# Graph attention with one-hot counts: destination one-hots compared twelve chunks at a time, three source one-hots a block made by ScalarE

## The chip, the cores and the metric

The kernel runs on one core of a Trainium2 chip. A core has TensorE (PE, matrix products), VectorE (DVE), ScalarE (ACT, activations), GpSimd (POOL) and DMA queues that SyncE (SP) feeds. Each engine takes its own instructions in order; semaphores make one wait for another. The metric is the device time of one execution in microseconds, the median of three runs.

## The reference

The reference normalises 1250 rows of 768 values, sends them through two graph attention layers (eight heads of 128, then one head of 768), adds the result, and puts a feed-forward network with a routed part for six rows behind it. Cut to the attention layer that the change is about:

```python
h = (x @ W.T).reshape(n, heads, out_ch)
e = leaky_relu(a_src[src] + a_dst[dst], 0.2)          # one value per edge and head
m = segment_max(e, dst);  ex = exp(e - m[dst])
alpha = ex / (segment_sum(ex, dst)[dst] + 1e-16)
out = segment_sum(alpha[:, :, None] * h[src], dst)
```

There are 21250 edges, sorted by destination. The kernel doesn't work on edges: it counts, for each pair of destination and source, how many edges join them (a 1250 x 1250 matrix), and then computes attention densely with the counts as factors.

## The kernel before, in words

**Tiles.** Nodes are in 10 blocks of 125 (`NB`, `B`). Edges are in 170 chunks of 125 (`EC`), 17 to a block (`CPB`); edge j of a chunk sits on partition j. `src_f` and `dst_f` hold source and destination of each edge as columns, one per chunk.

**The count stage (0 to about 160 us).** `count_block(b)` accumulates in PSUM the count matrix of destination block b. For each chunk it needs two one-hot matrices, made by `hot_chunk`: `of`, 125 edges x 1250 sources, and `to`, 125 edges x up to 96 destinations. A matmul with `to` (32 columns of it, a quarter of the block) as weights and `of` as the moving matrix, in three column pieces of 512, 512 and 226, adds the chunk's edges to the quarter (L294). Since edges are sorted, each quarter only needs a window of chunks (`WINDOWS`, with a margin of two), and `steps_of` puts chunks of the four quarters side by side; from block 7 on there are twelve steps. A runtime check (`edges_outside`, `n_val`) guards the windows; its other branch, `count_all`, isn't run with these data.

`of` is a compare of the iota row `node` with a column of `src_f`, on VectorE (`one_hot`, L219), 170 of them. It is written to one of twelve slots of `ring`, or to a block of `absent` that isn't in use yet. `to` is a compare on GpSimd (63), on VectorE (10, in blocks 1 and 2), or on ScalarE in two instructions (97): Abs of node - dst (L273), then Relu of 1 - that (L276).

`use_count` evacuates a block: `full_w`, a copy of the counts to f16 on ScalarE (`act_copy`, L376); `absent`, a large value where there is no edge (ScalarE, L305); ten transposes on TensorE (L316) and two ScalarE copies to `ct`, the transposed counts. ScalarE does these in its own order with everything else it has.

**Beside the counts.** In block 0 the layer norm of x and the transposes to `xt` run. From block 3 on, each block issues one `h1_block` of head group 0 (six matmuls, L443, and a ScalarE copy), placed behind the newest count matmul with `issue_after`, and four maxima of `top_of_block` (eight in blocks 4 and 8 of the trace): VectorE subtracts `absent` from a row of source terms and takes the maximum (L557), which the softmax needs. After block 9 TensorE does the remaining h1 blocks, to about 200 us.

**Attention, from 200 us.** For each head and each of ten source blocks, `weights` makes a 125 x 1250 factor tile `pt` (three buffers): VectorE (L581), ScalarE's exp (L584), VectorE times the counts (L585). Ten matmuls (L749) use it. Between factors VectorE does the tops that are still open, of heads 5 to 7 for the most part (`top_steps`), and TensorE does h1 blocks of group 1 (in heads 0 to 3), `fold_att2` and `h2_part` matmuls (L726, from head 4 on). `finish_head` divides by the softmax sum and transposes (L661 to L675). Then come h2, the second layer (L905) and the feed-forward network.

**Order.** The program is written in the order above; a scheduler with priorities lays out each engine's list from it when the program is built, with tile buffers and `issue_after` as constraints. A changed tile or engine can therefore move other instructions of the same engine.

The lines that the change edits:

```python
to = ep.tile([B, 3 * QUART], BF16, tag="to", bufs=20, name=f"to{c}")
if c < 2 * CPB + MARGIN:
    eng = (nc.gpsimd, nc.scalar if c < CPB else nc.vector)[c % 2]
else:
    eng = (nc.gpsimd, nc.scalar, nc.scalar)[c % 3]
```

Of the kernel before, what the change touches and what calls it, by code (L numbers as in the profile page):

```python
# [25 lines left out]
F32 = mybir.dt.float32  # L26
BF16 = mybir.dt.bfloat16
F16 = mybir.dt.float16
I32 = mybir.dt.int32
U16 = mybir.dt.uint16  # L30
AF = mybir.ActivationFunctionType
OP = mybir.AluOpType
AX = mybir.AxisListType

N = 1250
# [7 lines left out]
B = 125  # L43
NB = N // B
EC = E // B
# [8 lines left out]
CPB = EC // NB  # L54
MARGIN = 2
QUART = 32
NQ = 4
# [10 lines left out]
def gnn_ffn(  # L68
# [25 lines left out]
    nc = tc.nc  # L94

    def pool(name, bufs=1, space=None, stack=ctx):
        if space is None:
            return stack.enter_context(tc.tile_pool(name=name, bufs=bufs, reuse_waits="tile"))
        return stack.enter_context(tc.tile_pool(name=name, bufs=bufs, space=space))
# [7 lines left out]
    def ps_mm(name):  # L107
        return mm_pool[0].tile([128, 512], F32, tag="mm", name=name)

    def ps_tr(name):  # L110
        return psum.tile([128, 512], F32, tag="tr", bufs=2, name=name)
# [16 lines left out]
    ep = pool("early", stack=early)  # L128
# [31 lines left out]
    for i in range(2):  # L160
# [3 lines left out]
    node = ep.tile([B, NW], F16, name="node")  # L164
    nc.gpsimd.iota(
        node, pattern=[[1, NW]], base=0, channel_multiplier=0, allow_small_or_imprecise_dtypes=True
    )
    src_f = ep.tile([B, EC], F32, name="src_f")
    nc.vector.tensor_copy(src_f, src_i)
    dst_f = ep.tile([B, EC], F32, name="dst_f")  # L170
    nc.vector.tensor_copy(dst_f, dst_i)
    minus_dst = ep.tile([B, EC], F32, name="minus_dst")
    nc.vector.tensor_scalar(minus_dst, dst_f, -1.0, None, op0=OP.mult)

    first_i = ep.tile([B, NB, CPB], I32, name="first_i")
    last_i = ep.tile([B, NB, CPB], I32, name="last_i")

    def quarters_of(r):

        return [  # L180
            NQ * o + j for o in (-1, 0, 1) for j in range(NQ)
            if WINDOWS[j][0] <= r - CPB * o < WINDOWS[j][1]
        ]

    def start_of(quarter):
        return quarter // NQ * B + quarter % NQ * QUART

    for t, bounds in (
        (first_i, [start_of(quarters_of(r)[0]) for r in range(CPB)]),
        (last_i, [start_of(quarters_of(r)[-1] + 1) for r in range(CPB)]),  # L190
    ):
        c0 = 0
        for c1 in range(1, CPB + 1):
            if c1 == CPB or bounds[c1] != bounds[c0]:
                nc.gpsimd.iota(
                    t[:, :, c0:c1], pattern=[[B, NB], [0, c1 - c0]], base=bounds[c0],
                    channel_multiplier=0,
                )
                c0 = c1

    absent = marks.tile([B, NB, N], BF16, tag="marks", name="absent")
    ct = gpool.tile([B, NB, N], U16, name="ct")
    ones = ep.tile([B, 1], F32, name="ones")
# [14 lines left out]
    def one_hot(t, col, nodes):  # L218
        return nc.vector.tensor_scalar(t, nodes, col, None, op0=OP.is_equal)  # L219
# [23 lines left out]
    ring = ep.tile([B, 12, N], BF16, name="ring")  # L243
# [7 lines left out]
    hot = {}  # L251
    newest = {}

    def hot_chunk(c):

        quarters = [q + c // CPB * NQ for q in quarters_of(c % CPB)]
        quarters = [q for q in quarters if 0 <= q < NQ * NB]
        of = place_of[c]
        newest["of"] = one_hot(of, src_f[:, c : c + 1], node[:, :N])
        n0 = start_of(quarters[0])  # L260
        w = start_of(quarters[-1]) + QUART - n0
        to = ep.tile([B, 3 * QUART], BF16, tag="to", bufs=20, name=f"to{c}")
        if c < 2 * CPB + MARGIN:
            eng = (nc.gpsimd, nc.scalar if c < CPB else nc.vector)[c % 2]
        else:
            eng = (nc.gpsimd, nc.scalar, nc.scalar)[c % 3]
        if eng is not nc.scalar:
            eng.tensor_scalar(  # L268
                to[:, :w], node[:, n0 : n0 + w], dst_f[:, c : c + 1], None, op0=OP.is_equal
            )  # L270
            return of, to, n0
        away = ep.tile([B, 3 * QUART], F16, tag="away", bufs=1, name=f"away{c}")
        nc.scalar.activation(  # L273
            away[:, :w], node[:, n0 : n0 + w], AF.Abs, bias=minus_dst[:, c : c + 1], scale=1.0
        )
        nc.scalar.activation(to[:, :w], away[:, :w], AF.Relu, bias=ones, scale=-1.0)  # L276
        return of, to, n0

    def count_block(b, between={}):


        p = ps_count(f"count{b}")
        for i, step in enumerate(steps_of(b)):
            for _, c, _, _ in step:
                if c not in hot:
                    hot[c] = hot_chunk(c)
            if i in between:
                between[i]()
            for c0 in range(0, N, 512):
                c1 = min(N, c0 + 512)  # L290
                for j, c, first, last in step:
                    of, to, n0 = hot[c]
                    o = start_of(NQ * b + j) - n0
                    newest["count"] = nc.tensor.matmul(  # L294
                        p[QUART * j : QUART * (j + 1), c0:c1], to[:, o : o + QUART], of[:, c0:c1],
                        start=first, stop=last,
                    )
        use_count(p[:B, :N], b, f"w{b}", F16)

    def use_count(c, b, name, kind=F32):  # L300


        full = ep.tile([B, N], kind, tag="full", bufs=1, name=f"full_{name}")
        act_copy(full, c)
        nc.scalar.activation(absent[:, b], full, AF.Relu, bias=big_pos, scale=-ABSENT)  # L305
        if kind == F32:
            transpose_blocks(
                lambda g, m: ct[:, g : g + m, b * B : (b + 1) * B],
                lambda i: full[:, i * B : (i + 1) * B],
                NB, B, B, 4, f"ctp_{name}", act_copy,  # L310
            )
            return
        for g in range(0, NB, NB // 2):
            p = psum.tile([128, 8, 128], F16, tag="tr", bufs=2, name=f"ctp_{name}_{g}")
            for i in range(NB // 2):
                nc.tensor.transpose(  # L316
                    p[:B, i, :B], full[:, (g + i) * B : (g + i + 1) * B], ident16[:B, :B]
                )
            act_copy(ct[:, g : g + NB // 2, b * B : (b + 1) * B], p[:B, : NB // 2, :B])
# [22 lines left out]

    def edges_outside():

        below = ep.tile([B, EC], F32, name="below")
        outside = ep.tile([B, EC], F32, name="outside")
        n_out = ep.tile([B, 1], F32, name="n_out")
        nc.vector.tensor_tensor(below, dst_f, first_i.rearrange("p b c -> p (b c)"), OP.is_lt)
        nc.vector.tensor_tensor(outside, dst_f, last_i.rearrange("p b c -> p (b c)"), OP.is_ge)
        nc.vector.scalar_tensor_tensor(  # L350
            outside, outside, 1.0, below, op0=OP.mult, op1=OP.add, accum_out=n_out
        )
        n_p = ps_tr("n_out_p")
        nc.tensor.matmul(n_p[:1, :1], n_out, ones, start=True, stop=True)
        n_i = ep.tile([1, 1], I32, name="n_i")
        nc.vector.tensor_copy(n_i, n_p[:1, :1])
        return nc.values_load(n_i[:1, :1], min_val=0, max_val=E)
# [7 lines left out]
    def transpose_blocks(dst_of, src_of, n, rows, cols, per, name, evac):  # L365

        for g in range(0, n, per):
            m = min(per, n - g)
            p = ps_tr(f"{name}_{g}")
            pv = p[:cols, : m * rows].rearrange("p (c j) -> p c j", c=m)  # L370
            for i in range(m):
                nc.tensor.transpose(pv[:, i, :], src_of(g + i), ident[:rows, :rows])  # L372
            evac(dst_of(g, m), pv)

    def act_copy(o, i):
        nc.scalar.activation(o, i, AF.Copy)  # L376
# [90 lines left out]
    p = ps_tr("vp")  # L467
# [19 lines left out]
    p = ps_mm("a1p")  # L487
# [117 lines left out]
    for b in range(1, NB):  # L605
        count_block(b)
        if b == 2:
            n_val = edges_outside()
        if b == 3:
            new_group()  # L610
        if b >= 3:
            with tc.issue_after(newest["count"].ins):
                h1_block(0, b - 3)
        first_tops(behind.get(b, ()), range(4))
        if b == 5:
            attention_columns()
            as1_lo, as1_hi = low_high(a1[:, 0], [B, H1, NB], "as1")
# [161 lines left out]
    p = ps_mm("a2p")  # L779
# [13 lines left out]
    p = ps_tr("a2tp")  # L793
# [101 lines left out]
    for q in range(NB // 2):  # L895
        pt = pt2[q]
        for i in range(2):
# [14 lines left out]
            for g in (1, 0):  # L912
                c = slice(g * 384, (g + 1) * 384)
# [4 lines left out]
        c = slice(2 * q, 2 * q + 2)  # L918
# [142 lines left out]
    for r1, r0 in ((0, 3), (1, 4), (2, None)):  # L1061
        pair = [(1, r1)] if r0 is None else [(1, r1), (0, r0)]
        for m in range(KH):
            for r, a in pair:
                for g in range(2):
                    q = 32 * (2 * (1 - r) + g)
# [6 lines left out]
    for r in range(2):  # L1073
        for g in range(2):
            q = 32 * (2 * (1 - r) + g)
            c = slice(g * 384, (g + 1) * 384)
# [67 lines left out]
```

## Time and profile before

| | us |
|---|---|
| median of three runs | 787.17 (786.72 to 787.53) |
| the profiled execution | 786.1 |
| its span, first to last instruction | 784.3 |
| TensorE busy | 745.2 |
| VectorE busy | 580.0 |
| ScalarE busy | 323.7 |
| GpSimd busy | 121.1 |
| block 8's and block 9's `full_w` start | 145.25, 157.40 |
| first attention matmul | 200.57 |

How to read it: "busy" sums the time in which an engine has an instruction running, so it says where the work is, not what waits for what. The chain that ended last follows the work back from the last instruction, at each step to what released it. A group's row gives line, engine and operation, output<-input with shape, how many, busy time and mean nanoseconds of one, then the idle time of the engine just before them and what ended it. A wait's row gives who waited for whom, the sum in us, how often, and the longest. Matmul rows count two records for each fp32 matmul.

### The profile page before, as it was taken

The page shows a single profiled execution, that of the slowest core. Times are in us where ns is not written, and L with a number is a line of the kernel's source. Part 1 is how long each engine was busy: PE and PEld are TensorE (multiplying, and loading weights), DVE is VectorE, ACT ScalarE, POOL GpSimd, SP SyncE. Part 2 cuts the span into 40 slices and gives each one's busy share as a digit, 9 for nine tenths or more (in the row PEclk, how much of TensorE's full clock was granted, in tenths as well). Part 3 has the DMA queues.
Part 4 walks back from the last instruction along what each step waited for, and adds up shares of the span by engine and source line. Part 5 has one row for each costly group of instructions (what it writes and reads, how often), then busy time and mean ns, then how long its engine had stood idle before and what let it go on. Part 6 is the DMA issues. An engine that isn't in the chain of part 4 may idle for free.

```text
span 784.3 us, 11527 instructions
## 1 busy us (share of the span) xinstructions
PE 745.2 (95%) x4612; PEld 493.4 (63%) x4612; DVE 580.0 (74%) x974; ACT 323.7 (41%) x589; POOL 121.1 (15%) x104
## 2 busy tenths in 40 slices
PE   4988998999989999899999999999999999999997
PEld 1553443544777777788888888455555555576755
DVE  7859999999999999999878785297856622251412
ACT  4989987522355546453635462202331300011000
POOL 5236677200000000000000000100010101023010
PEclk9999999899999999999999999999999999999999
DMA  9651000017002020422220100402211001094811
GB/s 238 217 207 41 3 1 1 2 67 242 37 2 67 1 67 1 147 81 67 81 67 1 67 1 2 152 0 69 64 36 31 29 20 40 0 316 111 329 40 40
DMA packets 21553, 58.49 MB, mean 75 GB/s; under 512 B 2385, under 2 KB 7627, under 8 KB 20344
## 3 DMA queue, kind: packets, MB, share of 16 engines
q1 hardware_dynamic: 21496, 57.72, 22.3%
q8 instruction: 37, 0.61, 0.3%
q14 instruction: 20, 0.16, 0.1%
HBM read 53.74 MB, written 3.98 MB: 74 GB/s over the span
## 4 chain that ended last, share of the span: by engine, by line
PE 60%; DVE 13%; issue 3%; ACT 2%; ACTq 0%; DVEq 0%
PE acc L905 15%; PE h2p L726 13%; PE acc L749 12%; DVE pt L581 6%; PE f L970 5%; PE f L954 5%; DVE pt L585 5%; PE h1p L443 4%; DVE unused L557 2%; PE h1tp L674 1%; ACT on L671 1%; PE a2p L782 1%; PE xt2p L372 1%; PE candp L1067 1%; PE v2p L696 1%
## 5 line engine op out<-in xcount | busy, mean ns | idle before, releaser
L584 ACT ACTIVATE pt<-pt,as_lo 125x1250 f32<-125x1250 f32 (+1 forms) x130 | 128.0, 1012 | 202.7 <-DVE pt L581 188.1
L749 PEld LDWEIGHTS acc<-g,pt 125*125 125x125 f32 x1600 | 185.0, 188 | 25.3 <-DVE pt L585 17.5
L749 PE MATMUL acc<-g,pt 125*125 125x129 f32 x1600 | 191.8, 275 | 7.1 <-DVE pt L585 7.1
L585 DVE SCALAR_TENSOR_TENSOR pt<-pt,ct 125x1250 f32<-125x1250 f32 (+1 forms) x130 | 133.2, 1053 | 11.9 <-ACT pt L584 11.5
L905 PE MATMUL acc<-h,pt 125*125 125x385 f32 (+1 forms) x400 | 129.7, 486 | 0.0
L581 DVE SCALAR_TENSOR_TENSOR pt<-rows_h,as_hi 125x1250 f32<-125x1250 f32 x80 | 119.8, 1514 | 11.0 <-PE acc L749 10.8
L443 PE MATMUL h1p<-w1s,xt 128*125 128x512 f32 x240 | 109.2, 597 | 0.6 <-ACT g L376 0.5
L905 PEld LDWEIGHTS acc<-h,pt 125*125 125x125 f32 x400 | 74.6, 187 | 53.9
L726 PE MATMUL h2p<-w2s,g 128*125 128x384 f32 x320 | 107.4, 487 | 0.0
L268 POOL TENSOR_SCALAR to<-node,dst_f 125x64 bf16<-125x64 f16 (+4 forms) x63 | 80.1, 1471 | 50.7 <-PE count L294 48.7
L726 PEld LDWEIGHTS h2p<-w2s,g 128*125 128x125 f32 x320 | 58.1, 187 | 37.7 <-issue 0.9
L294 PE MATMUL count<-ring,to 125*32 125x512 bf16 (+1 forms) x729 | 69.6, 362 | 6.4 <-DVE ring L219 5.3
L443 PEld LDWEIGHTS h1p<-w1s,xt 128*125 128x125 f32 x240 | 42.7, 188 | 47.4 <-issue 45.6
L294 PEld LDWEIGHTS <-to 125*32 125x32 bf16 x1068 | 37.7, 99 | 53.6 <-issue 23.8
L901 POOL TENSOR_TENSOR xb<-xb,b2r 125x768 f32<-125x768 f32 x10 | 18.5, 1850 | 326.0 <-DVE a_row L787 180.4
L219 DVE TENSOR_SCALAR ring<-node,src_f 125x1250 bf16<-125x1250 f16 x116 | 59.7, 545 | 7.0 <-PE count L294 4.5
L294 PE MATMUL count<-absent,to 125*32 125x512 bf16 (+1 forms) x339 | 52.4, 361 | 8.8 <-POOL to L268 6.6
L557 DVE CUSTOM_DVE_ANT_0 unused<-rows,absent 125x1250 bf16<-125x1250 f32 x40 | 58.0, 1449 | 0.4 <-DVEq L622 0.3
L557 DVE CUSTOM_DVE_ANT_0 unused<-srow_h,absent 125x1250 bf16<-125x1250 f32 x40 | 58.1, 1452 | 0.2
L974 DVE TENSOR_TENSOR o<-f,o 125x384 f32<-125x384 f32 x20 | 11.1, 557 | 52.5 <-PE f L970 27.4
L970 PE MATMUL f<-wf,gt 128*125 128x384 f32 x120 | 39.5, 486 | 0.0
L276 ACT ACTIVATE to<-away,ones 125x64 bf16<-125x64 f16 (+4 forms) x97 | 33.9, 349 | 13.3 <-PE count L294 9.4
(176 smaller groups left out, 619.5 us busy)
## 6 DMA issues: line engine op xcount, KB each, us to landing
rows_h<-r_h_d SPq DMA_DIRECT2D x8, 1250.0 KB
w_more<-in_atom_in_t SPq DMA_DIRECT2D x3, 1152.0 KB
w_more<-in_atom_out_t SPq DMA_DIRECT2D x3, 1152.0 KB
x<-in_x SPq DMA_DIRECT2D x10, 336.0 KB
xb<-in_x SPq DMA_DIRECT2D x10, 336.0 KB
srow_h<-as_d SPq DMA_DIRECT2D x5, 625.0 KB
w1n<-in_w SPq DMA_DIRECT2D x2, 1536.0 KB
w1s<-in_w1t SPq DMA_DIRECT2D x2, 1536.0 KB
```

Of the source, the lines that this page charges most:

```text
L219: return nc.vector.tensor_scalar(t, nodes, col, None, op0=OP.is_equal)
L268: eng.tensor_scalar(to[:, :w], node[:, n0 : n0 + w], dst_f[:, c : c + 1], None, op0=OP.is_equal)
L294: newest["count"] = nc.tensor.matmul(p[QUART * j : QUART * (j + 1), c0:c1], to[:, o : o + QUART], of[:, c0:c1], start=first, stop=last,)
L443: nc.tensor.matmul(p[:B], xt[:, k, b * B : (b + 1) * B], w1s[g][:, k], start=(k == 0), stop=(k == KD - 1),)
L557: nc.vector.tensor_tensor_reduce(out=unused, in0=hd.src_row, in1=absent[:, b], scale=1.0, scalar=-ABSENT, op0=OP.subtract, op1=OP.max, acc ...
L581: nc.vector.scalar_tensor_tensor(o, hd.rows[:, 0, c0:c1], hi, hd.rows[:, 1, c0:c1], op0=OP.add, op1=OP.max)
L584: nc.scalar.activation(o, o, AF.Exp, bias=lo, scale=1.0)
L585: nc.vector.scalar_tensor_tensor(o, o, 1.0, ct[:, s, c0:c1], op0=OP.min, op1=OP.mult)
L726: nc.tensor.matmul(p[:B, :384], groups[i][:, h, b * B : (b + 1) * B], w2h[i][:, h, g * 384 : (g + 1) * 384], start=(h == 0), stop=(h == 3),)
L749: nc.tensor.matmul(acc[g][:B, j * (C1 + 1) : (j + 1) * (C1 + 1)], pt[:, d * B : (d + 1) * B], h1v[h // 4][:, h % 4, s, :], start=(s == 0 a ...
L905: nc.tensor.matmul(acc[g][:B, : c1 - c0], pt[:, s, i * B : (i + 1) * B], h2[:, s, c0:c1], start=(s == 0), stop=(s == NB - 1),)
L970: nc.tensor.matmul(p[:B, :384], gt[:, m, i, :], wf2[:, m, c], start=(m == 0), stop=(m == KH - 1),)
```

## The change

A block's chunks are numbered r = 0 to 16. For the twelve chunks of `AT_ONCE`, whose destinations all fall in a window of 64, VectorE makes the destination one-hots in one compare per block, 125 x 768 elements: the row `near` (0 to 63) repeated, against twelve columns of `dst_near` (destination minus the start of the window), each repeated 64 times. The other five chunks' `to` are all on GpSimd. In blocks 3 to 9, chunks 4, 9 and 13 have their source one-hot made by ScalarE, Abs and then Relu over 1250 columns, instead of by VectorE. `minus_dst` goes, two tiles of `edges_outside` become bf16, and the unused branch of `use_count` takes its buffer from `ring`.

```diff
-    minus_dst = ep.tile([B, EC], F32, name="minus_dst")
-    nc.vector.tensor_scalar(minus_dst, dst_f, -1.0, None, op0=OP.mult)
...
+    AT_ONCE = (2, 3, 4, 5, 7, 8, 9, 10, 11, 12, 13, 14)
+    near = ep.tile([B, 2 * QUART], F16, name="near")
+    nc.gpsimd.iota(
+        near, pattern=[[1, 2 * QUART]], base=0, channel_multiplier=0,
+        allow_small_or_imprecise_dtypes=True,
+    )
+    dst_near = ep.tile([B, NB, len(AT_ONCE)], F16, name="dst_near")
+    for r0, r1, i in ((2, 6, 0), (7, 15, 4)):
+        nc.vector.tensor_sub(
+            dst_near[:, :, i : i + r1 - r0],
+            dst_f.rearrange("p (b c) -> p b c", c=CPB)[:, :, r0:r1], first_i[:, :, r0:r1],
+        )
...
+    def destinations_at_once(b):
+        t = ep.tile([B, len(AT_ONCE), 2 * QUART], BF16, tag="to_near", bufs=2, name=f"near{b}")
+        near_of[b] = t
+        shape = [B, len(AT_ONCE), 2 * QUART]
+        nc.vector.tensor_tensor(
+            t, near.unsqueeze(1).to_broadcast(shape),
+            dst_near[:, b].unsqueeze(2).to_broadcast(shape), OP.is_equal,
+        )
...
+        if r in AT_ONCE and b not in near_of:
+            destinations_at_once(b)
         of = place_of[c]
-        newest["of"] = one_hot(of, src_f[:, c : c + 1], node[:, :N])
+        if b >= 3 and r in (4, 9, 13):
+            away = ep.tile([B, N], F16, tag="away", bufs=1, name=f"away{c}")
+            nc.scalar.activation(
+                away, node[:, :N], AF.Abs, bias=src_f[:, c : c + 1], scale=-1.0
+            )
+            nc.scalar.activation(of, away, AF.Relu, bias=ones, scale=-1.0)
+        else:
+            newest["of"] = one_hot(of, src_f[:, c : c + 1], node[:, :N])
+        if r in AT_ONCE:
+            return of, near_of[b][:, AT_ONCE.index(r)], b * B + start_of(quarters_of(r)[0])
         n0 = start_of(quarters[0])
         w = start_of(quarters[-1]) + QUART - n0
-        to = ep.tile([B, 3 * QUART], BF16, tag="to", bufs=20, name=f"to{c}")
-        if c < 2 * CPB + MARGIN:
-            eng = (nc.gpsimd, nc.scalar if c < CPB else nc.vector)[c % 2]
-        else:
-            eng = (nc.gpsimd, nc.scalar, nc.scalar)[c % 3]
-        if eng is not nc.scalar:
-            eng.tensor_scalar(
-                to[:, :w], node[:, n0 : n0 + w], dst_f[:, c : c + 1], None, op0=OP.is_equal
-            )
-            return of, to, n0
-        away = ep.tile([B, 3 * QUART], F16, tag="away", bufs=1, name=f"away{c}")
-        nc.scalar.activation(
-            away[:, :w], node[:, n0 : n0 + w], AF.Abs, bias=minus_dst[:, c : c + 1], scale=1.0
-        )
-        nc.scalar.activation(to[:, :w], away[:, :w], AF.Relu, bias=ones, scale=-1.0)
+        to = ep.tile([B, 3 * QUART], BF16, tag="to", bufs=10, name=f"to{c}")
+        nc.gpsimd.tensor_scalar(
+            to[:, :w], node[:, n0 : n0 + w], dst_f[:, c : c + 1], None, op0=OP.is_equal
+        )
         return of, to, n0
...
-        full = ep.tile([B, N], kind, tag="full", bufs=1, name=f"full_{name}")
+        if kind == F32:
+            full = ring[:, 2:4].rearrange("p i n -> p (i n)").bitcast(F32)
+        else:
+            full = ep.tile([B, N], kind, tag="full", bufs=1, name=f"full_{name}")
...
-        below = ep.tile([B, EC], F32, name="below")
-        outside = ep.tile([B, EC], F32, name="outside")
+        below = ep.tile([B, EC], BF16, name="below")
+        outside = ep.tile([B, EC], BF16, name="outside")
```

## The prediction

> **What bounds the kernel now.** I read the page's busy shares first, then the chain that ended last, then a table by stage, then the waits and groups of the stage that the change edits. Share and chain:
>
> ```profile
> PE 745.2 (95%) x4612; PEld 493.4 (63%) x4612; DVE 580.0 (74%) x974; ACT 323.7 (41%) x589; POOL 121.1 (15%) x104
> PE 60%; DVE 13%; issue 3%; ACT 2%; ACTq 0%; DVEq 0%
> ```
>
> TensorE is busy 95% of the span, so there is little to win unless its idle time or the order of its work changes. The table by stage shows where that idle time is:
>
> ```profile
> core 0: us, PE busy (x) PEld busy (x) DVE busy (x) ACT busy (x) POOL busy (x), PEclk, DMA share, GB/s
> 0.00:56.00 56.00, 41.52 (x438) 21.23 (x442) 40.88 (x117) 41.09 (x87) 19.46 (x44) 0.94 0.68 213
> 56.00:160.00 104.00, 94.59 (x972) 47.53 (x961) 103.44 (x194) 82.57 (x193) 64.83 (x39) 0.97 0.05 19
> 160.00:200.00 40.00, 39.37 (x93) 16.92 (x92) 39.50 (x69) 10.41 (x13) 0.17 (x1) 1.00 0.45 153
> 200.00:330.00 130.00, 122.85 (x864) 100.61 (x863) 129.28 (x136) 64.38 (x85) 0.12 (x1) 1.00 0.14 48
> 330.00:560.00 230.00, 228.55 (x1370) 169.12 (x1369) 179.52 (x241) 95.45 (x158) 3.61 (x2) 1.00 0.17 55
> ```
>
> The change edits the count stage, which ends with the tenth block's count at 157.4 us. From 56 us on VectorE has no gap there (103.44 of 104), and it stays full to 330. TensorE is full from 160 to 200 (h1 blocks), waits for VectorE's attention factors from 200 to 330, and has no gap from 328 on. So VectorE microseconds saved before 160 come out at the end only through TensorE's start into attention, or through factors that arrive earlier between 200 and 330. The waits of 56 to 160, and the chain where VectorE hands over to TensorE:
>
> ```profile
> POOL to L268 <- PE count L294: 31.8, 10, 6.6
> ACT to L276 <- PE count L294: 9.4, 4, 6.7
> ACT full_w L376 <- PE count L294: 6.6, 3, 5.6
> PEld L294 <- ACT to L276: 3.9, 8, 0.7
> PE count L294 <- DVE ring L219: 3.0, 3, 1.5
> ```
>
> ```profile
> 323.58 2.95 DVE pt L581 x2
> 328.03 4.67 PE acc L749 x40
> ```
>
> GpSimd waits 31.8 us for TensorE: not a bound. ScalarE waits 16 us for TensorE, so it has room on average, not necessarily at each place. The durations that I use, by groups kept apart by shape:
>
> ```profile
> L219 DVE TENSOR_SCALAR ring<-node,src_f 125x1250 bf16<-125x1250 f16 x116 | 59.7, 545 | 7.0 <-PE count L294 4.5 <-PE vt L455 2.5
> L557 DVE CUSTOM_DVE_ANT_0 unused<-rows,absent 125x1250 bf16<-125x1250 f32 x40 | 58.0, 1449 | 0.4 <-DVEq L622 0.3
> L273 ACT ACTIVATE away<-node,minus_dst 125x64 f16<-125x64 f16 x70 | 24.3, 347 | 5.1 <-DVE minus_dst L173 3.1
> L305 ACT ACTIVATE absent<-full_w,big_pos 125x1250 bf16<-125x1250 f16 x10 | 13.3, 1329 | 0.0
> L376 ACT ACTIVATE full_w<-count 125x1250 f16<-125x1250 f32 x10 | 12.0, 1203 | 6.6 <-PE count L294 6.6
> ```
>
> Back to back, starts are nearer than durations: 0.457 us for a one-hot, 1.38 for a top, 0.38 for a ScalarE instruction of 64 columns, 1.1 for full_w.
>
> [...] a GpSimd one-hot takes 0.72 us beside an idle VectorE and 2.16 (median) from 56 to 160. [...]
>
> **The change part by part.** (1) VectorE, before 56 us. minus_dst (-0.17) goes; two small subtractions (+0.27) and block 0's compare come. A compare has 768 columns: from the trace's two-source 125x170 instruction, 0.24 from start to start[...]. Sum +0.96, ahead of the layer-norm scale that ScalarE waits for, but ScalarE no longer makes 0.38 us instructions in pairs there (minus_dst alone cost it 3.1 of waiting): nil or better. Blocks 1 and 2: two compares (1.73) for ten VectorE destination one-hots (1.7): nil. full_w of blocks 1 and 2 no longer queues behind ScalarE pairs (TensorE waited 2.58 and 1.85 there): the saturated phase starts about 0.4 earlier.
> (2) VectorE, blocks 3 to 9: ScalarE takes 21 source one-hots; 20 fall into the gap-free phase: -20 x 0.457 = -9.1. Compares: +6 x 0.865 = +5.2. Net -3.9. [...]
> (3) ScalarE per block: before, about 11.3 pairs x 0.76 = 8.6, plus full_w, absent, two ct copies and the h1 copy, 4.0: 12.6. After, 3 x (1.33 + 1.36) = 8.1 plus 4.0: 12.1. Blocks last 12.2 to 20.3 us, so it fits in total. But the pieces are long, and the instruction order of the changed kernel, fixed when the program is built, puts the ninth and thirteenth chunk's pair behind the previous block's full_w, absent, ct and h1 copy. With T the start of full_w, the third one-hot ends at about T + 8.3 (blocks 5, 7) and T + 9.4 (6, 8); TensorE needs it at T + 8.7 to T + 10. In block 9 the list is full_w 1.1, Abs 1.36, absent 1.33, ct 1.26, h1 copy (not before TensorE's h1 block at T + 6.0) 0.6, Relu, Abs, Relu 4.1: T + 10.7. TensorE wants it in the sixth of twelve steps, T + 8.7, so some 2 us are lost; the remaining steps take 3.6: the count ends at T + 14.3 where before it was 12.15.
> (4) Sum of the stage. Block 8's count: 145.25 - 0.4 - 18 x 0.457 + 6 x 0.865 = 141.8, with 0.4 lost to slots 142.2; block 9's: 142.2 + 14.3 = 156.5 against 157.40. TensorE then does the same 40 us of h1 blocks; its first attention matmul moves from 200.57 to 199.6: -0.97. VectorE's own gain is not lost at once (it has done more tops by then), but its fourth factor needs a buffer that TensorE's first attention group frees (it waited 0.19 for that at 202.97), so both start 0.97 early.
> (5) What moves later. The last 24 tops still have to be done between the factors (22 in the changed kernel, two more before the first). In the instruction order, tops done ahead of a factor, counted on from the kernel before's first factor (before / after): factor 30 15/15, factor 32 15/17, 40 18/21, 44 19/23, 50 24/24. Up to four tops (4 x 1.38 = 5.5 us) move from head 4, where VectorE has slack (1.7 to 3.8 us), into heads 2 and 3 and the start of 4, where TensorE waits for it; in TensorE's order three h2 matmuls and the att2 fold move ahead a little as filler. I wrote both orders forward with the trace's steps (factor parts 1.43 and 1.39, exp 1.1, top 1.38, an attention matmul 0.22, h2 0.645, h1 0.867), three factor buffers and six PSUM buffers. For before this puts head 7's first transposition at 493.6; the trace has 492.4. TensorE's idle in each stretch, before to after: 230 to 265 1.7 to 1.35, 265 to 350 8.3 to 11.5, 350 to 500 4.9 to 4.3. Net +2.2; with durations varied by a few hundredths, +1.9 to +2.6. After head 4 the two orders are the same work, TensorE gap-free.
> (6) bf16 for the two outside-edge tiles, the iota on GpSimd, fewer buffers: no wait in the trace stands on them, nil; with GpSimd late at the start, +0.3 at most.
> Sum: -0.97 + 2.2 = +1.2. On the profiled 786.1 (span 784.3 and 1.8 around it) 787.3; the median of the runs is 1.07 higher, so 787.17 + 1.2 = 788.4.
>
> **The rivals.** A, likeliest: as above, 788.4, own range 786.5 to 790; for it speaks the gap-free TensorE from 328, against it that a wait of 2 us in block 9 is read off a list. B, the saving survives: no ScalarE wait in block 9, its count ends at 153.5 (-3.9), and the compare costs less or the tops move harmlessly (+0.5 to +1.5): -2.4 to -4, about 784. It needs the count's end before 153.6; for it, the 103.44 of 104, against it the order in (5). B', block 9 without a wait but (5) as reckoned: -1.5, 785.7. C, slower: ScalarE sets the pace. Blocks 5, 6, 7 and 9, four tops each, took 51.6 together. If the third one-hot lands at T + 10.4 instead of T + 8.3 to 9.4 (a longer wait for the single away buffer, or a later h1 copy), each takes 14.0, 56.0 together: +4.4, less 1.9 saved elsewhere (0.4 at the start, and nine one-hots against three compares in blocks 3, 4 and 8): the count ends 2.4 later, with (5) +4.6, 791.8. It decides from 13.4 a block, where the count's end no longer comes earlier. A fourth, nothing reaches the end: VectorE idles the gain away in front of 200.57 and (5) costs half: 788.
>
> **How the numbers follow.** A 0.45, B 0.15, B' 0.10, C 0.25, nothing 0.05. About 0.2% (1.57 us) is what a measurement can tell from no change, 785.6 to 788.7. A lies 0.25 within and 0.20 above; B faster; B' 0.05 and 0.05; C slower; the last within. Faster 0.20, same 0.35, slower 0.45. The likeliest is 788.4; 8 in 10 reaches from B's upper part, 784.3, to C, 791.8.
>
> **What would show it.** The compare's row at about 0.87 from start to start, six of them in the saturated phase; 1250-wide Abs and Relu at 1.33; full_w of block 8 near 142 and of block 9 near 156.5 with a wait of TensorE for ScalarE's one-hot in block 9; first attention matmul near 199.6; TensorE's waits for factors between 265 and 350 up by about 3. It is wrong if block 9's count ends before 154 (then B or B'), if blocks 5 to 8 show TensorE waiting for ScalarE each time (C), or if waits from 265 to 350 are no longer than now.

## The result, and the profile after

The changed kernel takes 789.14 us (median of 17 executions, 787.51 to 791.79) against 787.53 for the kernel before in the same comparison (786.05 to 788.86): a ratio of 1.0023, with a 95% interval of 1.0013 to 1.0033. It is slower by about 1.8 us. 788.4 was predicted. The profiled execution took 787.51, the shortest of the 17; its span of 785.7 is 1.4 above the one before, and the readings below account for that 1.4, not for the 1.8 of all executions.

Shares and chain of the changed kernel (in its listing every line number after the count stage is 26 higher: L775 is L749, L583 is L557, L607 and L611 are L581 and L585):

```profile
PE 743.4 (95%) x4612; PEld 497.0 (63%) x4612; DVE 578.3 (74%) x954; ACT 312.3 (40%) x437; POOL 103.4 (13%) x92
...
PE 62%; DVE 11%; issue 3%; ACT 2%; ACTq 0%; DVEq 0%
```

VectorE lost only 1.7 us of busy time in all. The table by stage, columns as before the change:

```profile
0.00:56.00 56.00, 43.22 (x490) 21.76 (x490) 44.66 (x117) 31.53 (x51) 22.57 (x43) 0.97 0.67 208
56.00:160.00 104.00, 92.93 (x919) 49.98 (x919) 101.20 (x180) 82.38 (x78) 44.14 (x28) 0.93 0.06 22
160.00:200.00 40.00, 39.38 (x106) 17.94 (x105) 39.45 (x68) 9.75 (x12) 0.17 (x1) 1.00 0.45 153
200.00:330.00 130.00, 120.21 (x844) 99.85 (x844) 128.57 (x137) 63.77 (x84) 0.12 (x1) 0.99 0.14 48
```

Two things stand out. VectorE has done 44.66 us of work by 56 us, 3.8 more than before: it got going earlier. And between 200 and 330 TensorE is busy 2.6 us less than before while VectorE is as full as it was: TensorE waits more for it there.

The milestones say where the time went. Block 8's full_w starts at 140.37 (before 145.25), block 9's at 154.89 (157.40), the first attention matmul at 198.05 (200.57). So 2.5 us are saved where attention begins. A factor is one `pt` tile; they are numbered 0 to 79 over the eight heads, and a time given for one is the start of its first attention matmul. The lead holds to factor 16 (251.50 against 254.01) and is lost between factors 18 and 44: factor 24 is 2.06 ahead, but with three h1 matmuls still to do that the kernel before has behind it there; at factor 28, with those done, the lead is 0.07; factor 36 is 1.59 late, factor 44 1.46 late (355.99 against 354.53), and that stays to the end of the heads (492.23 against 490.81). After 200 us 3.9 us are lost. TensorE's waits for factors between 200 and 350 us (sum, how often, longest), in the kernel before and in the changed one:

```profile
PE acc L749 <- DVE pt L585: 7.1, 9, 1.5
```

```profile
PE acc L775 <- DVE pt L611: 9.7, 7, 3.0
```

The new operations cost what was reckoned. By groups kept apart by shape:

```profile
L271 DVE TENSOR_TENSOR near<-near,dst_near 125x768 bf16<-125x768 f16 x10 | 9.5, 953 | 0.0
...
L286 ACT ACTIVATE away<-node,src_f 125x1250 f16<-125x1250 f16 x21 | 28.0, 1335 | 1.9 <-POOL near L201 1.6
```

The compare has 0.87 from its start to the next instruction's (64.77 to 65.64), and the ScalarE instructions 1.34.

### The profile page after: what moved, and what is told of

It reads as the page before. It is cut to its first block, busy times and chain, and to the rows that moved or that the text cites. A ratio compares the mean times of both kernels' runs of the same rounds, so it can differ in the third digit from the quotient of the medians.

```text
span 785.7 us, 11306 instructions
## 1 busy us (share of the span) xinstructions
PE 743.4 (95%) x4612; PEld 497.0 (63%) x4612; DVE 578.3 (74%) x954; ACT 312.3 (40%) x437; POOL 103.4 (13%) x92
## 4 chain that ended last, share of the span: by engine, by line
PE 62%; DVE 11%; issue 3%; ACT 2%; ACTq 0%; DVEq 0%
PE acc L931 15%; PE acc L775 14%; PE h2p L752 13%; PE f L996 5%; PE f L980 5%; PE h1p L469 5%; DVE pt L607 5%; DVE pt L611 4%; DVE unused L583 2%; PE h1tp L700 1%; PE a2p L808 1%; ACT on L697 1%; PE xt2p L398 1%; PE v2p L722 1%; PE candp L1093 1%
## 5 line engine op out<-in xcount | busy, mean ns | idle before, releaser
L775 PEld LDWEIGHTS acc<-g,pt 125*125 125x125 f32 x1600 | 186.4, 189 | 26.9 <-DVE pt L611 16.8
L775 PE MATMUL acc<-g,pt 125*125 125x129 f32 x1600 | 192.4, 276 | 9.8 <-DVE pt L611 9.7
L611 DVE SCALAR_TENSOR_TENSOR pt<-pt,ct 125x1250 f32<-125x1250 f32 (+1 forms) x130 | 133.5, 1054 | 13.3 <-ACT pt L610 12.8
L607 DVE SCALAR_TENSOR_TENSOR pt<-rows_h,as_hi 125x1250 f32<-125x1250 f32 x80 | 120.3, 1514 | 13.2 <-PE acc L775 13.1
L297 POOL TENSOR_SCALAR to<-node,dst_f 125x61 bf16<-125x61 f16 (+4 forms) x50 | 62.9, 1361 | 57.6 <-PE count L317 52.4
L317 PE MATMUL count<-ring,near 125*32 125x512 bf16 (+1 forms) x474 | 55.4, 373 | 4.7 <-DVE ring L230 2.2
L583 DVE CUSTOM_DVE_ANT_0 unused<-rows,absent 125x1250 bf16<-125x1250 f32 x40 | 58.1, 1452 | 0.4 <-DVEq L648 0.3
L583 DVE CUSTOM_DVE_ANT_0 unused<-srow_h,absent 125x1250 bf16<-125x1250 f32 x40 | 58.1, 1454 | 0.2
L317 PE MATMUL count<-ring,to 125*32 125x512 bf16 (+1 forms) x255 | 52.2, 362 | 2.9 <-DVE ring L230 2.9
L317 PEld LDWEIGHTS <-near 125*32 125x32 bf16 x720 | 32.8, 103 | 34.0 <-issue 19.9
L230 DVE TENSOR_SCALAR ring<-node,src_f 125x1250 bf16<-125x1250 f16 x99 | 50.3, 543 | 4.3 <-PE count L317 4.3
L317 PE MATMUL count<-absent,near 125*32 125x512 bf16 (+1 forms) x246 | 42.2, 384 | 10.1 <-DVE near L271 7.1
L317 PEld LDWEIGHTS <-to 125*32 125x32 bf16 x348 | 28.5, 101 | 18.1 <-issue 9.1
```

The source lines that it names most:

```text
L297: nc.gpsimd.tensor_scalar(to[:, :w], node[:, n0 : n0 + w], dst_f[:, c : c + 1], None, op0=OP.is_equal)
L317: newest["count"] = nc.tensor.matmul(p[QUART * j : QUART * (j + 1), c0:c1], to[:, o : o + QUART], of[:, c0:c1], start=first, stop=last,)
L583: nc.vector.tensor_tensor_reduce(out=unused, in0=hd.src_row, in1=absent[:, b], scale=1.0, scalar=-ABSENT, op0=OP.subtract, op1=OP.max, acc ...
L607: nc.vector.scalar_tensor_tensor(o, hd.rows[:, 0, c0:c1], hi, hd.rows[:, 1, c0:c1], op0=OP.add, op1=OP.max)
L611: nc.vector.scalar_tensor_tensor(o, o, 1.0, ct[:, s, c0:c1], op0=OP.min, op1=OP.mult)
L775: nc.tensor.matmul(acc[g][:B, j * (C1 + 1) : (j + 1) * (C1 + 1)], pt[:, d * B : (d + 1) * B], h1v[h // 4][:, h % 4, s, :], start=(s == 0 a ...
```

## The experiments

In each comparison below the kernel before was run again beside the variant. Its medians were 786.52 in the comparison of the first four, 787.62 in that of the next four and 787.17 in the last, so ratios are the safer figure. Halved stretches are those in which the trace shows half the granted TensorE clock.

**1. The changed kernel with the tops where the kernel before has them.** The count stage is the changed one. Each top from the seventh of heads 5 to 7 on is tied behind one factor part:

```diff
             if s in top_steps.get(h, ()):
-                tops.pop(0)()
+                n = 3 * NB - len(tops)
+                if n in BEHIND:
+                    k, part = BEHIND[n]
+                    with tc.issue_after(factor[k][part].ins):
+                        tops.pop(0)()
+                else:
+                    tops.pop(0)()
```

> The changed kernel, with the tops of the attention stage held behind the same factor parts as in the kernel before, so that VectorE's list from the first factor on is that of before; the count stage is the changed one. Theory (order): the count stage's gain of 2.5 us reaches the first attention matmul, and the loss of 3.9 us after it comes from the tops' new places; then the first attention matmul stays near 198.0, every factor stays about 2.5 ahead of before, and the time is 2.5 below before, some 785.0, about 4 below the changed kernel. Rival (the clock, or where tiles lie): the loss of 3.9 stays with the old order, and the time is that of the changed kernel, 789.

Measured: 783.04, ratio 0.9956 (0.9942 to 0.9969). The first attention matmul is at 197.53, and the lead over the kernel before is 3.0 at every factor from 0 to 70, without a step. TensorE's waits for factors between 200 and 350 are as before:

```profile
PE acc L813 <- DVE pt L611: 7.1, 9, 1.5
```

So the loss after 200 us goes with the order of the tops, and the count stage's gain is real. From the first attention matmul on TensorE's list is that of the kernel before again too, instruction by instruction; in the changed kernel some h1 and h2 matmuls and a few attention matmuls stand elsewhere. The run puts both lists back at once and doesn't separate them.

**2. The kernel before with the tops as early as the changed kernel has them.**

> The kernel before with nothing of the change, but with the tops of the attention stage issued as early as the changed kernel has them (eight ahead of the first factor, the others behind and ahead of the same factor parts; some factor parts swap places with it, so the list is near to the changed kernel's but not the same). Theory (order): the count stage is as before, the first attention matmul stays at 200.6, and the time rises by 2 to 5 us (written forward as in the prediction this list costs 3.9): 790 to 792. Rival: the order of the tops costs nothing, 787.5.

Measured: 796.19, ratio 1.0121 (1.0105 to 1.0136), 9.7 above. The direction is the theory's, the size is twice what was expected. Of the 10.9 us by which its last attention matmul is late, 1.3 are there at the first one, 6.5 are more waiting of TensorE (13.6 against 7.1), and two halved stretches of 3.4 us, at 275.0 and 350.0, may make up most of the rest. This list was not the changed kernel's own (factor parts trade places in it, and head 7's source row is loaded earlier), so the run shows that a list of this kind is dear, not what this change's order costs.

**3. Tops in the old order, and block 9's third one-hot on VectorE.**

```diff
-        if b >= 3 and r in (4, 9, 13):
+        if b >= 3 and r in ((4, 9, 13) if b < 9 else (4, 9)):
```

> As the run with the tops held in the old order, and in block 9 the one-hot of chunk 13 is VectorE's again (ScalarE keeps chunks 4 and 9). Theory: TensorE's wait of 1.9 us for ScalarE's third one-hot in block 9 goes, VectorE pays 0.46 for it, the tenth count ends about 1.5 earlier (153.4), and so does the run: 783.5. Rival: the wait passes to the next late thing in that block (a VectorE one-hot, or the second of ScalarE): no difference from that run, 785.0.

Measured: 781.15, ratio 0.9941 (0.9928 to 0.9955). ScalarE's timeline of the changed kernel, block 9 (start, duration, instruction, and in brackets the idle time before it and what ended it), and the one TensorE row that waits in it:

```profile
140.37 1.21 ACT L402 ACTIVATE full_w<-count 125x1250 f16<-125x1250 f32 x1
141.47 1.33 ACT L286 ACTIVATE away<-node,src_f 125x1250 f16<-125x1250 f16 x1
142.70 1.32 ACT L331 ACTIVATE absent<-full_w,big_pos 125x1250 bf16<-125x1250 f16 x1
143.93 1.26 ACT L402 ACTIVATE ct<-ctp_w 125x625 uint16<-125x625 f16 x2
146.34 0.60 ACT L402 ACTIVATE g<-h1p 125x512 f32<-125x512 f32 x1 [1.15 <-PE h1p L469]
147.03 1.34 ACT L289 ACTIVATE ring<-away,ones 125x1250 bf16<-125x1250 f16 x1
148.40 1.34 ACT L286 ACTIVATE away<-node,src_f 125x1250 f16<-125x1250 f16 x1
149.77 1.34 ACT L289 ACTIVATE ring<-away,ones 125x1250 bf16<-125x1250 f16 x1
154.89 1.21 ACT L402 ACTIVATE full_w<-count 125x1250 f16<-125x1250 f32 x1 [3.78 <-PE count L317]
```

```profile
151.16 0.39 PE L317 MATMUL count<-ring,near 125*32 125x512 bf16 x2 [1.88 <-ACT ring L289]
```

The order is the predicted one: the third one-hot ends 10.7 after block 8's full_w, TensorE waits 1.88 for it, and block 9 takes 14.52. In the run without that third one-hot:

```profile
139.20 1.21 ACT L402 ACTIVATE full_w<-count 125x1250 f16<-125x1250 f32 x1
...
145.86 1.34 ACT L289 ACTIVATE ring<-away,ones 125x1250 bf16<-125x1250 f16 x1
...
151.52 1.21 ACT L402 ACTIVATE full_w<-count 125x1250 f16<-125x1250 f32 x1 [4.32 <-PE count L317]
```

Block 9 takes 12.32 here, 2.2 less, and nothing else took the wait's place. The median fell by 1.9 against the first run; the intervals of the two ratios overlap, so the size rests on the two profiles.

**4. Tops in the old order, all source one-hots on VectorE.** The condition on ScalarE's one-hots is never met (`b >= NB`).

> As the run with the tops held in the old order, but all source one-hots are VectorE's again: the compare of twelve chunks alone. Theory (VectorE's sum sets the count stage): 20 one-hots of 0.457 come back (9.1) and ScalarE's waits in block 9 go; against before VectorE has 5.2 more, less 0.4 to 1 at the start: the tenth count ends 4 later than before, near 161.5, and the time is 791.5. Rival (TensorE or ScalarE set the stage, the compare is hidden): within 1.5 of before.

Measured: 789.04, ratio 1.0037 (1.0024 to 1.0049), first attention matmul 202.89, 2.3 later than before. The theory's sign holds, its 4 was too much. Blocks 1 and 2 end at 48.50 and 56.39, 1.7 and 3.2 earlier than before, where 0.4 to 1 had been allowed. What TensorE waited for between 29 and 57 us, before and here:

```profile
PE ctp_w L316 <- ACT full_w L376: 2.6, 1, 2.6
PE xtp L372 <- ACT xt L376: 0.7, 1, 0.7
```

```profile
PE ctp_w L342 <- ACT full_w L402: 1.4, 1, 1.4
```

The new way of making destination one-hots is thus worth 3 us at block 2 by itself. That ScalarE's part in it counts most is read from these waits and not shown alone: the same edit takes ten destination one-hots off VectorE in blocks 1 and 2, and the kernel before has a halved stretch in block 2 (51.0 to 54.4) that this run doesn't have.

**5. Only the last six tops held.** The changed kernel, with `BEHIND` of the first run cut to tops 24 to 29.

> The changed kernel, its count stage untouched; of the tops of the attention stage only the last six are held behind the factor parts where the kernel before has them (factors 43 to 49), the others stay where the changed kernel puts them. Theory (the tops moved out of head 4 carry the loss): the time falls to that of the run with all tops in the old order, 783, or a little lower; written forward this list is 2.0 better than the old one: 781. Rival (the earlier tops, of heads 0 to 2, carry it): 787 to 789.

Measured: 784.6, ratio 0.9964 (0.9950 to 0.9977). From factor 28 to 44 this run gains 2.0 on the kernel before, where the changed kernel loses 1.5: that is the part that the tops moved out of head 4 carry. From factor 18 to 28 it still loses, as the changed kernel does. So the loss has two places, and neither the theory nor the rival had it whole. The second is at factor 20, where the new list puts the first part of factor 22 ahead of the second part of factor 21, and TensorE has no h1 matmul to do meanwhile. TensorE's timeline there, the changed kernel first, then the kernel before:

```profile
267.92 0.79 PE L775 MATMUL acc<-g,pt 125*125 125x129 f32 x2 [2.98 <-DVE pt L611]
```

```profile
267.12 2.49 PE L749 MATMUL acc<-g,pt 125*125 125x129 f32 x18 [1.00 <-DVE pt L585]
```

And around it the granted clock (the third column from the end) of the changed kernel:

```profile
262.00:267.00 5.00, 2.63 (x22) 2.24 (x20) 5.00 (x9) 1.82 (x2) 0.00 (x0) 1.00 0.00 0
267.00:271.00 4.00, 3.08 (x14) 3.08 (x15) 3.70 (x4) 3.17 (x10) 0.00 (x0) 0.57 0.00 0
271.00:276.00 5.00, 5.00 (x47) 4.93 (x46) 4.77 (x5) 3.75 (x7) 0.00 (x0) 1.00 0.01 3
```

In the four microseconds after the wait TensorE had 0.57 of its clock; one attention matmul (two records) takes 0.79 there. In this fifth run the halved stretch at the same wait is 6.8 long.

**6. Tops in the old order, ScalarE with two source one-hots in every block.**

> As the run with the tops held in the old order, and ScalarE keeps two source one-hots a block (chunks 4 and 9) in all blocks, 14 instead of 21. Theory (VectorE's sum sets the stage up to block 8, ScalarE only block 9): against the run that changes block 9 alone VectorE has six one-hots of 0.457 more, 2.7 us: 783.9. Rival (ScalarE's third pair sets the pace in the other blocks too): as fast as that run or faster, 781 or less.

Measured: 783.09, ratio 0.9943 (0.9929 to 0.9957). The run of the same comparison that changes block 9 alone (the next one) has 781.65, so giving ScalarE's third one-hot back in blocks 3 to 8 costs 1.4 in the medians. The two intervals overlap, while single executions took 782.5 to 783.9 and 781.4 to 782.8; block 8's full_w, 3.3 later than in the third run, points the same way. ScalarE doesn't set the pace of the stage as a whole, though it does in block 3: from block 2's full_w to block 3's there are 13.1 us in the third run and 10.3 here, where this wait of the third run is missing:

```profile
PE count L317 <- ACT absent L289: 2.8, 1, 2.8
```

VectorE does tops meanwhile and is idle for less than 0.1 us there in the third run; block 4 is 3.2 longer here (16.0 against 12.7), and at block 7's end the two are level (121.57 and 121.47). All of the 3.3 comes in block 8.

**7. The one-line edit of block 9 alone, nothing held.** The edit of the third run on the changed kernel. The scheduler's list then has the tops where the kernel before has them, but for one that moves ahead of the first factor.

> The changed kernel with nothing held; only block 9's third one-hot is VectorE's. In the list that the scheduler then writes, the tops stand ahead of the factors as in the kernel before. Theory (the places of the tops count, not the holding of them): the time of the run with this edit and the tops held, 781.2. Rival (holding them did something of its own): 785 or more.

Measured: 781.65, ratio 0.9925 (0.9912 to 0.9938), TensorE's waits between 200 and 350 again 7.1 us in nine. One VectorE instruction more in block 9 brings back the old order of the tops in heads 0 to 5, with that one exception, and TensorE's old list whole. This version is faster than both kernels.

**8. The edit of block 9, and the tops held where the program writes them.**

> Block 9's third one-hot on VectorE, and the tops from the ninth on held behind the factor where the program writes them, so that six fall between factors 0 and 40 instead of eighteen, the rest in heads 4 to 6. Theory (tops between the factors of heads 0 to 3 delay TensorE, those behind cost nothing): TensorE's waits for factors of 7.1 between 200 and 350 shrink; written forward 1.8 better than the old list: 779.4. Rival (they make the factors of heads 4 and 5 late instead): 782 or more.

Measured: 783.44, ratio 0.9951 (0.9935 to 0.9967): the theory's 779.4 was missed. VectorE is busy 115.6 of the 130 us from 200 to 330 here, 14 less, and the lead grows from 3.0 to 6.9 by factor 16. But TensorE waits as long, 7.2 us, and 1.80 at the second factor of heads 1, 2 and 3; two of these waits go with halved stretches (265.4, 303.0), and the late tops crowd heads 4 and 5 (factor 42 is 2.1 late). Less work for VectorE there is not enough; what its list has at a head's start counts.

**9. The wait at factor 20 filled.** The changed kernel with its own list of tops and three matmuls more, which no result uses:

```diff
+                if (h, s, d) == (2, 0, 5):
+                    idle = ps_tr("idle")
+                    with tc.issue_after(product.ins):
+                        for k in range(3):
+                            nc.tensor.matmul(
+                                idle[:B], xt[:, k, :B], w1s[1][:, k], start=(k == 0), stop=(k == 2)
+                            )
```

> The changed kernel with its own list of tops, and three more matmuls of 512 columns into an unused tile (some 2.6 us, no result uses them), placed where TensorE waits 2.98 us for the second factor of head 2 and its clock is halved for 3.4 us from 267.6 on; TensorE's list differs in these three alone. Theory (the halving goes with the wait): no halved stretch there, TensorE gains up to 1.7 us, and from factor 24 on it is about 1.5 ahead of the changed kernel: 787.5. Rival (the halving has another cause and comes by itself): halved there all the same, and the time stays at 789 or rises.

Measured: 786.34, ratio 0.9988 (0.9979 to 0.9997). TensorE's timeline of this run:

```profile
266.06 2.74 PE L820 MATMUL idle<-w1s,xt 128*125 128x512 f32 x6
269.21 0.48 PE L811 MATMUL acc<-g,pt 125*125 125x129 f32 x2 [0.41 <-DVE pt L611]
```

and its clock:

```profile
268.00:272.00 4.00, 3.59 (x25) 2.67 (x24) 3.97 (x5) 4.00 (x12) 0.00 (x0) 1.00 0.00 0
```

With TensorE busy through the wait, the halved stretch is gone, and the first matmul behind it takes 0.48 instead of 0.79. In its profile, which entered factor 20 1.29 behind the changed kernel's, it has caught up by factor 22. So the halving cost 1.3 us, and work without a use made the kernel faster. By the ratios the run is 2.8 us below the changed kernel (0.9988 against 1.0023), more than 1.3. The single executions point to where the rest may be. Six of the changed kernel's 17 have a mean granted clock of 0.983 and took 789.93 to 791.79; the other eleven, the profiled one among them, have 0.986 to 0.989 and took 787.51 to 789.47. All 14 of this run have 0.988 or more. A mean clock lower by 0.004 over 787 us is, as an estimate, 6.3 us more at half clock, about two stretches; where they lie no profile shows.

## Why the prediction was right, and where by luck

The time lies 0.7 from the predicted one and in its range, and what happened is its likeliest case: the saving at the count's end is given back in heads 2 to 4. Its single terms fared differently.

**VectorE's sum (2).** The compare was reckoned at 0.865, an estimate of the author's, and has 0.87; the one-hots are as before. Right. The trace of before alone gives as much: from start to start a two-source instruction of 170 columns takes 0.24 and a top of 1250 columns 1.38, which puts 768 columns, as an estimate, at 0.87. One reading beside it was wrong: the GpSimd one-hot of 0.72 us isn't beside an idle VectorE, for a one-source one-hot of VectorE's covers 58% of it. What the trace does show: in the kernel before, 64-column one-hots on GpSimd take 2.19 us (median of 27) where they overlap a two-source VectorE instruction and 0.84 (median of 18) where they don't.

**The start of the saturated phase (1).** This is the term that was mis-sized: 0.4 earlier was predicted. VectorE's idle time between 29 and 57 us fell from 10.7 to 7.0, and block 2's count ends 3.0 earlier. The prediction named the right wait, TensorE's 2.58 for block 1's full_w behind ScalarE's pairs, but booked 0.4 for the phase without a working. That wait fell to 1.40, the 0.7 for `xt` went, and block 2's full_w, also named, was waited for as long as before (1.78 against 1.85). The fourth run shows that the new destination one-hots alone bring the 3 us, not which engine's share in them.

**Block 9 (3).** Right in mechanism and size: T + 10.7 for the third one-hot, a wait of 1.88 for "some 2", 14.52 for 14.3; and the runs bear out a cost of some 2 us: the third run's profile has 2.2 less in block 9, and the seventh run's ratio of 0.9925 lies clear of the first run's 0.9956. The prediction had block stages of 12.2 to 20.3 us and so ScalarE's 12.1 always fitting; block 3 was missing from that, with 10.6 before. There TensorE waits 2.4 us for ScalarE's one-hot and the stage grows to 14.3, but VectorE does two tops more meanwhile, and block 4 is 2.7 shorter.

**The count's end (4).** Because of the earlier start it moved by 2.5, not 0.97 (the predicted 156.5 against 157.40 is in fact 0.9): block 8's full_w came at 140.37, not 142.2.

**The order of the tops (5).** The mechanism is shown by the first run. Written forward it was 2.2; it is 3.9 in the profile. TensorE's idle time from 230 to 350 grew by 3.0 (5.0 to 8.0), close to the 2.85 written forward, though that started from 10.0. The 0.6 that was to come back between 350 and 500 didn't (1.45 and 1.44). The clock that was halved from the 2.98 us wait on cost 1.3, as the ninth run shows; the halving was left out of the reckoning altogether. From the first attention matmul to the last the idle time grew by 3.3, so with the clock there are 4.6, and 0.7 of that is offset by something that the profiles don't name. The place was half right: heads 2 to 4 as predicted, but 2.4 of it from factor 16 to 28, at a head's start, and 1.5 from 28 to 44, the part that the prediction explained by tops moved out of head 4.

Put together, in the profile: -2.5 at the first attention matmul and +3.9 after it make the +1.4 of the span, where -0.97 and +2.2 had been reckoned. The gain was 1.5 larger and the loss 1.7 larger than predicted; the total was near because these two errors nearly cancel, and that is luck.

Rival C, ScalarE setting the pace of the four-top blocks, fell: TensorE waits for a ScalarE one-hot 0.4 us in block 5 and not at all in 6, 7 and 8, and the sixth run is slower than the seventh. The times alone wouldn't rule it out: blocks 5, 6, 7 and 9 took 53.6 together, between the 51.6 of before and its 56.0. Rival B, the saving surviving, is what the kernel becomes once the order of the tops is put back.

What stays open: why the scheduler's list takes the other form with three ScalarE one-hots in block 9 and the old one with two; the runs show that it does, not what tips it.

## What to carry to other kernels

When a change alters an earlier stage, compare the whole instruction lists, not only the edited stage: where a scheduler fills gaps of its own reckoning, a saving in one stage can reorder another, and here that took back more than the saving. If the list got worse, tie the moved instructions to their old places before judging the edit; here it turned +0.23% into -0.44%. Look at the start of the next phase of a saturated engine too: which waits keep it from getting full.

## What the runs showed of the hardware

TensorE's clock was halved for stretches of 3.4 us or multiples of it: in the kernel before 3.41 us from 13.47, 3.41 from 51.02 and 6.83 from 136.35, in the changed kernel 3.41 from 14.97, 10.24 from 59.34, 3.41 from 134.44 and 3.41 from 267.56, each with 0.50 of the clock. Between 200 us and the last few it was halved only beside or within 1.2 us of a wait of TensorE. In the traces of both kernels the changes of the clock lie on one grid: in the kernel before they are 1, 10, 1, 24 and 2 times 3.413 us apart, in the changed kernel 1, 12, 3, 19, 1, 38 and 1 times; the second run's stretches at 275.0 and 350.0 are 22 steps apart, the eighth run's at 265.4 and 303.0 are 11. Waits of 2.98 and 2.99 (the changed kernel, the fifth run), 2.71 and 1.93 (the second) and two of three of 1.80 (the eighth) went with a halved stretch between 200 and 350; the third of 1.80, waits of 2.34 and 1.66 in the changed kernel, one of 2.36 in the second run and all of 1.5 and less did not.

Laid on the grid of their own trace, these waits sort themselves. Between 200 us and the last few, six windows of 3.413 us in which TensorE was idle for 1.80 us or more (1.80 twice in the eighth run, 1.93 and 2.71 in the second, 2.25 in the fifth, 2.62 in the changed kernel) were each followed by half clock, and no full-clock window with 1.72 or less was. The changed kernel's wait of 2.34 has a boundary inside, with 1.72 on one side of it. The second window of the fifth run's 6.8 us is the one case outside this: it follows a window already at half clock with 0.74 idle. In the ninth run TensorE, left unfilled, would have been idle from 266.22 to 269.21, some 2.4 us of it in one window (an estimate from its grid and the end of the wait), so it was the filling, not a grid that lay elsewhere, that kept the clock up. Before 160 us the same limit doesn't sort the windows: 1.85 idle from 57.84 on in the kernel before and 1.88 from 148.09 on in the changed kernel were not followed by half clock; why is open.

The early stretch was 3.4 long in the third run and, as an estimate from its mean clock of 0.91 up to 56 us, about 10 in the first; block 1's count ended at 48.45 in the third, at 49.85 in the first and at 50.87 in the seventh: a difference of up to 2.4 us between profiles with the same count stage up to there, which is more than some of the effects measured here. That is why the medians and ratios decide between variants, and differences of single profiles are read from the first attention matmul on.
